# Thirteen blocks of a four-layer kernel turned by block transfers and VectorE instead of TensorE

## The chip, the cores and the metric

The kernel runs on one core of a Trainium2 chip. A core has TensorE (PE: matmuls, with its weight loads shown as PEld), VectorE (DVE), ScalarE (ACT), GpSimd (POOL) and SyncE (SP), whose queue issues most DMAs. The metric is the device time of one execution in microseconds. The kernel before took 1141.09 us, the median of three runs (1140.71 to 1141.46).

## The reference, cut to what matters

The input is 2 sequences of 1024 tokens with 512 channels, all f32. Four layers follow one another, each with a residual sum and a layer normalisation over the channels:

```python
x = layernorm(x + mamba(x, W_in, conv, A_log, D, dt_bias, norm_w, W_out))   # 16 heads of 64, state 16
x = layernorm(x + linear(x, weight, scale))          # product, then a bound on each row's norm
x = layernorm(x + recurrent(x, w_y, w_x, conv, w_ig, w_ag, w_out, ...))     # gated linear recurrence
x = layernorm(x + swiglu(x, gate_w, up_w, down_w, scales))   # integer weights minus 128, 2048 hidden
```

Every layer multiplies x from the right by a weight. TensorE contracts over the partition axis, so each layer needs its input with channels on the partitions ("turned"). The residual sum and the normalisation need tokens on the partitions. So x is turned once per layer.

## The kernel before, in words

The 2048 tokens are four blocks of 512 (`NBLK` = 4, two per sequence). A block of x is kept as a tile of 128 partitions x 4 token groups x 512 channels, 1 MB. Turned, it is 128 partitions x 4 channel groups x 512 tokens.

**Turning.** `transposed` (L232) makes 16 TensorE transposes of 128x128 for a block, four into each of four PSUM banks. ScalarE (L241) or VectorE (L243) copies each bank out. With `split` it writes two pieces instead: ScalarE a rounded fp32r copy (L236) and VectorE the remainder (L237), because the linear layer and SwiGLU run their products as two fast fp32r matmuls in place of one f32 matmul. `by_channel` (L890, L893, L895) does the same for SwiGLU.

**Mamba.** `head(b)` turns block b, makes the small B, C and dt products, starts their convolution (`mix`) and for b > 0 works out the decays by rows (`by_rows`), which go through HBM (`decays`, `since`) and come back broadcast into L. `project(b)` makes the inner products, convolutions and scans (L535); `recur(b)` runs the four chunks (L663, L673, L694); `gates(b)` makes the gate products (L705); `conclude(b)` is the out-projection (L728) with residual and normalisation, and stores the block to `x_mid` in HBM. `weave` mixes one of these as the main line with steps of others: while block b recurs, block b - 1 concludes and head b + 1 runs. Block 0's start, `opening`, is written out by hand and keeps its order on TensorE, VectorE and ScalarE; in it two steps of head 1 are taken.

**Linear.** `linear(b)` loads x from `x_mid` in HBM, turns and splits it into two single-buffered pieces (named wu and wd in the trace, since they share those tags), multiplies (L909), evicts (L913), works out the norm's factor and adds it to x (L933). Blocks 0 and 1 are woven into the last `conclude`, blocks 2 and 3 into the first block of the recurrent layer.

**Recurrent.** `branches(b)` turns x and makes two products (L960) with a convolution and a GELU. `recurrence(b)` makes the two gates (L960, from cv), then a chain of ScalarE, VectorE and GpSimd work that ends in the scan hs (L1025) and y (L1031). `project_back(b)` is its out-projection (L1037) with residual and normalisation. The order is recurrence(b), project_back(b - 1), and the rest of branches(b + 1).

**SwiGLU.** `hidden(m)` makes gate and up products of hidden tile m (L1111, 16 matmuls: 4 channel groups x 2 pieces x 2 weights), then sg (ScalarE, L1118), h (VectorE, L1120), hh (ScalarE, L1126) and hl (VectorE, L1128). `down(m)` adds tile m's 8 down-products (L1134). down(m) is issued after hidden(m + 1). Between blocks, `by_channel(b + 1)` stands between down(14) and down(15). Weights of groups 1 to 3 are loaded and converted by GpSimd (L864) during block 0.

**Order.** Outside the sections ordered by hand the framework's planner orders each engine's instructions: it plays the program through with its own estimates of durations and takes, of what it thinks ready, what comes first in the program. `keep_in_program_order` pins an instruction behind all earlier ones of its engine. Each engine's queue then runs in that fixed order and waits at the first instruction that isn't ready. `reuse_waits="tile"` lets a tile that takes over memory wait for the old tile in that place alone.

Of the kernel before, what the change touches and what calls it, by code (L numbers as in the profile page):

```python
# [37 lines left out]
def model_kernel(ctx: ExitStack, tc: tile.TileContext, t: dict, out: bass.AP):  # L38
# [7 lines left out]
    x_mid = tc.dram_tile([NBLK, P, NJ, D], F32, name="x_mid")  # L46
# [174 lines left out]
    def transposed(pool, b, X, tags=("xT",), split=False, bufs=1, by_act=False):  # L221


        pieces = [
            pool.tile([P, NK, TB], F32R if split else F32, tag=tag, name=f"{tag}{b}", bufs=bufs)
            for tag in tags
        ]
        xT = pieces[0]
        for k in range(NK):
# [5 lines left out]
            if split:  # L235
                nc.scalar.copy(xT[:, k, :], pt)  # L236
                nc.vector.tensor_tensor(  # L237
                    pieces[1][:, k, :], pt, xT[:, k, :].bitcast(F32), ALU.subtract
                )
            elif k % 2 or by_act:  # L240
                nc.scalar.copy(xT[:, k, :], pt)  # L241
            else:
                nc.vector.tensor_copy(xT[:, k, :], pt)  # L243
        return pieces
# [16 lines left out]
    def causal_conv(acc, xpad, w):  # L261

        for k in range(3):
            nc.vector.scalar_tensor_tensor(  # L264
                acc, xpad[:, k : k + TB], w[:, k : k + 1], acc, ALU.mult, ALU.add
            )

# [31 lines left out]
    def started(pm, n, b, row, w, bias, dst, xpad):  # L299
# [10 lines left out]
        def rest():  # L310
            causal_conv(acc[:n, :], xpad[:n, :], w)
            nc.scalar.activation(dst, acc[:n, :], AF.Silu)
# [29 lines left out]
    def head(b, st):  # L342
# [4 lines left out]
        xT = st["xT"] = transposed(mp, b, X, bufs=2, by_act=b > 0)[0]  # L347
# [27 lines left out]
        if b:  # L375
            mix()
# [53 lines left out]
    def by_rows(b, turn, tk):  # L430
# [5 lines left out]
        )  # L436
        if b == 1:
            exponents(*(by_hj[:, i : i + 1] for i in range(1, 5)), pinned=True)
        bias, _, end, rA, rN = (by_hj[:, i : i + 1] for i in range(5))
        nc.vector.tensor_scalar(z, z, bias, None, ALU.add)  # L440
# [140 lines left out]
    def opening(st, own, g, coming):  # L581
# [35 lines left out]
        next(coming)  # L617
# [102 lines left out]
    def conclude(b, st):  # L720
# [27 lines left out]
        nc.sync.dma_start(x_mid[b], X[b])  # L748
# [12 lines left out]
    for b in range(NBLK):  # L761
        if b:
            g, coming = gates(b, st), {}
            fill, plan = conclude(b - 1, before), (0, 0, 2, 0, 2, 0, 2, 2)
            ahead = head(b + 1, coming) if b + 1 < NBLK else iter(())
# [3 lines left out]
        else:  # L769
            turns = (ahead, g, g, ahead, g, g)  # L770
            weave(recur(b, H, st), (next(steps, None) for steps in turns), (2, 2, 1, 1))
# [50 lines left out]
    def later_layers(exact, last=None):  # L822
# [10 lines left out]

        w_f0 = ep.tile([P, NK, D], F32, tag="wF", name="w_f0" + suffix)
        nc.sync.dma_start(w_f0, w_f0_source)
        for b in range(2):
            nc.sync.dma_start(X[b], x_mid[b])
        w1 = wp.tile([P, 5, NK, D], F32, tag="wA", name="w1" + suffix)  # L840
        f0s = par["f0s"] = row("L0_ffn_scale", D, c1, nc.sync, "scale")
        for i, name in enumerate(("w_x", "w_y")):
            nc.sync.dma_start(w1[:, i], w_sources[name])
        nc.sync.dma_start(X[2], x_mid[2])
# [40 lines left out]
        def by_channel(b, X, pieces):  # L885

            for k in range(NK):
                pt = bank("pt")
                for j in range(NJ):
                    nc.tensor.transpose(  # L890
                        pt[:, j * P : (j + 1) * P], X[b][:, j, k * P : (k + 1) * P], ident
                    )
                nc.scalar.copy(pieces[0][:, k, :], pt)  # L893
                if exact:
                    nc.vector.tensor_tensor(  # L895
                        pieces[1][:, k, :], pt, pieces[0][:, k, :].bitcast(F32), ALU.subtract
                    )

        def linear(b):

            xT = transposed(ep, b, X, tags=("wu0", "wd0") if exact else ("wu0",), split=exact)
# [35 lines left out]
            layernorm(X[b], engine=nc.gpsimd)  # L937
            yield

        if last:  # L940
            steps, free = last

            weave(steps, itertools.chain(linear(0), linear(1)), (0, 1, 0, 2, 0, 1, 0, 2, 1))
            free()
        else:
            for _ in itertools.chain(linear(0), linear(1)):
                pass
        nc.sync.dma_start(X[3], x_mid[3])
        for i, name in ((2, "w_ig"), (3, "w_ag"), (4, "w_out")):
# [350 lines left out]
```

## Time and profile before

| what | value |
|---|---|
| median of three runs | 1141.09 us |
| the profiled execution | 1140.83 us |
| its span | 1139.0 us |
| TensorE busy | 1116.2 us, 98% of the span |
| VectorE, ScalarE, GpSimd busy | 677.6, 466.1, 357.8 us |
| granted TensorE clock, mean | 0.998 |
| all transposes of x on TensorE | 256, in 16 groups of 16 |
| HBM read, written | 49.47 MB, 8.68 MB |

A row of the profile names line, engine, operation, output and inputs, shapes and count, then busy time and mean duration. A row of the timeline gives start, duration, engine, line, operation and count; in square brackets stands the idle time before it and what ended it. Matmuls overlap, so a single duration is longer than the step from one to the next.

### The profile page before, as it was taken

The page shows a single profiled execution, that of the slowest core. Times are in us where ns is not written, and L with a number is a line of the kernel's source. Part 1 is how long each engine was busy: PE and PEld are TensorE (multiplying, and loading weights), DVE is VectorE, ACT ScalarE, POOL GpSimd, SP SyncE. Part 2 cuts the span into 40 slices and gives each one's busy share as a digit, 9 for nine tenths or more (in the row PEclk, how much of TensorE's full clock was granted, in tenths as well). Part 3 has the DMA queues.
Part 4 walks back from the last instruction along what each step waited for, and adds up shares of the span by engine and source line. Part 5 has one row for each costly group of instructions (what it writes and reads, how often), then busy time and mean ns, then how long its engine had stood idle before and what let it go on. Part 6 is the DMA issues. An engine that isn't in the chain of part 4 may idle for free.

```text
span 1139.0 us, 12263 instructions
## 1 busy us (share of the span) xinstructions
PE 1116.2 (98%) x4610; PEld 681.3 (60%) x4610; DVE 677.6 (59%) x1226; ACT 466.1 (41%) x714; POOL 357.8 (31%) x347
## 2 busy tenths in 40 slices
PE   8999999999999999999999999999999999999996
PEld 5455445545544655654444444448888888888885
DVE  5997895696769676862707237083328765225224
ACT  3352634453453233566654372543223223223224
POOL 1547461573348240556123212237501001001000
PEclk9999999999999999999999999999999999999999
DMA  9004002401210047112000000003601001000001
GB/s 325 13 16 167 1 1 90 167 0 39 111 71 0 38 173 207 75 47 74 1 1 0 1 0 1 0 1 121 184 1 38 1 1 37 1 1 10 28 1 40
DMA packets 32732, 59.22 MB, mean 52 GB/s; under 512 B 11841, under 2 KB 12641, under 8 KB 30105
## 3 DMA queue, kind: packets, MB, share of 16 engines
q1 hardware_dynamic: 31464, 57.94, 14.6%
q8 instruction: 38, 0.62, 0.2%
q10 hardware_dynamic: 976, 0.39, 0.1%
q14 instruction: 30, 0.24, 0.1%
q0 software_dynamic: 224, 0.02, 0.0%
HBM read 49.47 MB, written 8.68 MB: 51 GB/s over the span
## 4 chain that ended last, share of the span: by engine, by line
PE 84%; DVE 10%; ACT 4%; issue 1%; DMA 1%; SPq 0%; DVEq 0%; ACTq 0%
PE pgu L1111 21%; PE p L960 17%; PE po L1134 10%; PE pg L336 9%; PE px L336 7%; PE po L728 6%; PE po L1037 4%; PE py L663 3%; DVE acc L264 2%; PE po L909 2%; DVE L L535 2%; PE pxt L632 1%; PE pt L232 1%; DVE xc L713 1%; PE py L655 1%
## 5 line engine op out<-in xcount | busy, mean ns | idle before, releaser
L1120 DVE SCALAR_TENSOR_TENSOR h<-pgu,L_ffn_up_scale,sg 128x512 f32<-128x512 f32 x64 | 47.9, 749 | 147.7 <-PE pgu L1111 143.5
L336 PE MATMUL px<-xT,w_in 128*128 128x512 f32 x256 | 114.6, 597 | 0.0
L550 POOL TENSOR_TENSOR L<-L,gm 128x512 f32<-128x512 f32 x64 | 93.5, 1490 | 66.9 <-DVE bdec L545 29.3
L728 PE MATMUL po<-w_out,xc 128*128 128x512 f32 x256 | 112.5, 593 | 2.1 <-DVE L L535 2.1
L336 PE MATMUL pg<-xT,w_in 128*128 128x512 f32 x256 | 113.5, 594 | 0.0
L960 PE MATMUL p<-xT,w 128*128 128x512 f32 x256 | 112.1, 592 | 1.4 <-ACT xT L241 1.4
L960 PE MATMUL p<-cv,w 128*128 128x512 f32 x256 | 111.0, 592 | 0.0
L1134 PE MATMUL po<-wd,hh 128*128 128x512 f32 x256 | 101.3, 396 | 0.0
L1111 PE MATMUL pgu<-wF__4423,wg 128*128 128x512 f32 x256 | 101.2, 396 | 0.0
L1134 PE MATMUL po<-wd,hl 128*128 128x512 f32 x256 | 101.0, 394 | 0.0
L1111 PE MATMUL pgu<-lo__4424,wg 128*128 128x512 f32 x256 | 100.7, 394 | 0.0
L1111 PE MATMUL pgu<-lo__4424,wu 128*128 128x512 f32 x256 | 100.7, 393 | 0.0
L1111 PE MATMUL pgu<-wF__4423,wu 128*128 128x512 f32 x256 | 100.7, 393 | 0.0
L1118 ACT ACTIVATE sg<-pgu,L_ffn_gate_scale 128x512 f32<-128x512 f32 x64 | 44.1, 689 | 132.9 <-PE pgu L1111 132.9
L1126 ACT CAST hh<-h 128x512 fp32r<-128x512 f32 x64 | 39.7, 621 | 117.6 <-DVE h L1120 117.4
L728 PEld LDWEIGHTS po<-w_out,xc 128*128 128x128 f32 x256 | 48.4, 190 | 63.1 <-issue 55.5
L960 PEld LDWEIGHTS p<-cv,w 128*128 128x128 f32 x256 | 48.4, 190 | 59.8 <-issue 58.6
L960 PEld LDWEIGHTS p<-xT,w 128*128 128x128 f32 x256 | 48.4, 190 | 58.8 <-issue 55.3
L336 PEld LDWEIGHTS px<-xT,w_in 128*128 128x128 f32 x256 | 47.6, 190 | 57.6 <-issue 56.7
L1241 POOL TENSOR_TENSOR x<-x,r 128x512 f32<-128x512 f32 x12 | 15.2, 1295 | 206.1 <-DVE r L1240 206.1
L336 PEld LDWEIGHTS pg<-xT,w_in 128*128 128x128 f32 x256 | 47.3, 190 | 54.2 <-issue 53.3
L264 DVE SCALAR_TENSOR_TENSOR acc<-xpad,cols,acc 128x512 f32<-128x512 f32 x72 | 67.5, 941 | 18.5 <-ACT acc L306 14.8
(279 smaller groups left out, 1934.5 us busy)
## 6 DMA issues: line engine op xcount, KB each, us to landing
L<-decays SPq DMA_DIRECT2D x12, 1024.0 KB, 8.3
x_mid<-x SPq DMA_DIRECT2D x4, 1024.0 KB, 3.9
x<-x_mid SPq DMA_DIRECT2D x4, 1024.0 KB, 7.2
st<-in_L_ffn_gate_w_dram SPq DMA_DIRECT2D x8, 512.0 KB, 4.7
st<-in_L_ffn_up_w_dram SPq DMA_DIRECT2D x8, 512.0 KB, 3.9
st<-in_L_ffn_down_w_dram SPq DMA_DIRECT2D x8, 512.0 KB, 3.7
x<-_attn_hidden_states_dram SPq DMA_DIRECT2D x3, 1024.0 KB, 16.6
out_dram<-x SPq DMA_DIRECT2D x3, 1024.0 KB, 4.3
```

The lines of the kernel that those rows point to most:

```text
L264: nc.vector.scalar_tensor_tensor(acc, xpad[:, k : k + TB], w[:, k : k + 1], acc, ALU.mult, ALU.add)
L336: nc.tensor.matmul(pm[:n, :], w_in[:, k, lo : lo + n], xT[:, k, :], start=(k == 0), stop=(k == NK - 1),)
L550: nc.gpsimd.tensor_tensor(L[:, h, :], L[:, h, :], st["gm"], ALU.mult)
L663: nc.tensor.matmul(pys[i][hh * HD : (hh + 1) * HD, q, :], dtx[q][:, 2 * i + hh, :], L[:, h, s], start=(first and q == 0), stop=(q == 1), s ...
L728: nc.tensor.matmul(po, xc[:, m, j * P : (j + 1) * P], w_out[:, m, :], start=(m == 0), stop=(m == NX - 1),)
L960: nc.tensor.matmul(pm, w1[:, i, k, m * P : (m + 1) * P], rhs[:, k, :], start=(k == 0), stop=(k == NK - 1),)
L1037: nc.tensor.matmul(po, y[:, k, j * P : (j + 1) * P], w1[:, 4, k, :], start=(k == 0), stop=(k == NK - 1),)
L1111: nc.tensor.matmul(pm, w[g][:, k, cols], x[:, k, :], start=(k == 0 and x is pieces[0]), stop=(k == NK - 1 and x is pieces[-1]),)
L1118: nc.scalar.activation(sg, pgu[0], AF.Silu, scale=gs[:, m : m + 1])
L1120: nc.vector.scalar_tensor_tensor(h, pgu[1], us[:, m : m + 1], sg, ALU.mult, ALU.mult)
L1126: nc.scalar.copy(hh, h)
L1134: nc.tensor.matmul(po[j], x[:, j * P : (j + 1) * P], wd[m // GK][:, m % GK, :], start=(m == 0 and x is h[0]), stop=(m == NF - 1 and x is h ...
```

## The change

A block that is to be turned is read from HBM by four DMAs (`load_blocks`), one for each 32 partitions, such that every 32x32 square of it already lies in its final place but is not itself turned. Each DMA moves runs of 32 channels, 128 bytes. Then four VectorE instructions (`turn_blocks`), one per channel group of 128 x 512, turn all 32x32 squares. This is done for mamba blocks 2 and 3, all linear blocks, recurrent blocks 1 to 3, and all SwiGLU blocks. Mamba blocks 0 and 1 and recurrent block 0 stay with TensorE. The linear layer and SwiGLU then split from SBUF instead of PSUM. To have the rows in HBM, the outputs of the linear layer (blocks 1 to 3) and of the recurrent layer (all) are stored as well (`x_lin`, `x_rec`).

The recurrent layer's five weights become five tiles, whose places also take the waiting blocks. Gate and up products of SwiGLU's hidden tile 0 are issued before the last `project_back`. In `opening` only one step of head 1 is left; its other steps come at chosen chunks of `recur(0)`, with the first tap of `mix` and the first operation of `by_rows` pinned. The plan that weaves linear 1 is shortened, and its remaining steps go into the first recurrent block.

```diff
-    x_mid = tc.dram_tile([NBLK, P, NJ, D], F32, name="x_mid")
+    x_mid, x_lin, x_rec = (
+        tc.dram_tile([NBLK, TB, D], F32, name=name) for name in ("x_mid", "x_lin", "x_rec")
+    )
...
+    def load_blocks(dst, rows):
+        blocks = rows.rearrange("(n t) (k a c) -> a t k n c", t=32, k=NK, c=32)
+        for a in range(4):
+            nc.sync.dma_start(
+                dst[32 * a : 32 * a + 32].rearrange("t k (n c) -> t k n c", c=32), blocks[a]
+            )
+
+    def turn_blocks(dst, src=None, pinned=False):
+        for k in range(NK):
+            turned = nc.vector.transpose(dst[:, k, :], (src or dst)[:, k, :])
+            if pinned:
+                tc.keep_in_program_order(turned)
...
-        xT = st["xT"] = transposed(mp, b, X, bufs=2, by_act=b > 0)[0]
+        if b > 1:
+            xT = st["xT"]
+            turn_blocks(xT, pinned=True)
+        else:
+            xT = st["xT"] = transposed(mp, b, X, bufs=2, by_act=b > 0)
...
-            mix()
+            mix(b == 1)
...
+        shifted = nc.vector.tensor_scalar(z, z, bias, None, ALU.add)
         if b == 1:
-            exponents(*(by_hj[:, i : i + 1] for i in range(1, 5)), pinned=True)
+            tc.keep_in_program_order(shifted)
+            exponents(*(by_hj[:, i : i + 1] for i in range(1, 5)))
...
         later.pop(0)()
-        next(coming)
         for conv in later:
...
+            if b + 1 < NBLK:
+                by_blocks(b + 1, coming)
+                ahead = head(b + 1, coming)
             weave(project(b, st), fill, plan, rest=False)
...
-            turns = (ahead, g, g, ahead, g, g)
-            weave(recur(b, H, st), (next(steps, None) for steps in turns), (2, 2, 1, 1))
+            turns = (ahead, g, ahead, g, g, g, ahead)
+            weave(recur(b, H, st), (next(steps, None) for steps in turns), (2, 2, 1, 2))
...
+        mid = [staged(ep, "lo", x_mid[0], "mid0")]
         for b in range(2):
-            nc.sync.dma_start(X[b], x_mid[b])
+            nc.sync.dma_start(X[b], rows_mid[b])
+        mid.append(staged(wp, "w3", x_mid[1], "mid1"))
...
-            xT = transposed(ep, b, X, tags=("wu0", "wd0") if exact else ("wu0",), split=exact)
+            x = mid.pop(0)
+            turn_blocks(x)
+            xT = [
+                ep.tile([P, NK, TB], WT, tag=tag, name=f"{tag}{b}")
+                for tag in (("wu0", "wd0") if exact else ("wu0",))
+            ]
+            split(x, xT)
...
-            weave(steps, itertools.chain(linear(0), linear(1)), (0, 1, 0, 2, 0, 1, 0, 2, 1))
+            weave(steps, two, (0, 1, 0, 2, 0, 1, 0, 2), rest=False)
...
-                xT = transposed(rp, b, X, by_act=True)[0]
+                if b:
+                    xT = rp.tile([P, NK, TB], F32, tag="xT", name=f"xT{b}")
+                    turn_blocks(xT, lin.pop(0))
+                    if b + 1 < NBLK:
+                        lin.append(staged(ep, "lo", x_lin[b + 1], f"lin{b + 1}"))
+                else:
+                    xT = transposed(rp, b, X, by_act=True)
...
+            def first_pieces():
+                rec = staged(rp, "xT", x_rec[0], "rec0")
+                yield
+                turn_blocks(rec)
+                ...
+                split(rec, pieces)
+                yield
...
-            weave(branches(0, st), itertools.chain(linear(2), linear(3)), (1,) * 8)
+            weave(
+                branches(0, st), itertools.chain(two, linear(2), linear(3)),
+                (2, 1, 1, 1, 1, 1, 1, 1, 1),
+            )
...
-            by_channel(0, X, pieces)
+            first_hidden = gate_up(0)
             project_back(NBLK - 1, ys[-1])
...
+                    if m == 6 and not final:
+                        load_blocks(following, x_rec[b + 1])
+                    if m == 10 and not final:
+                        turn_blocks(following)
                     down(m, ready.pop(0), po, range(NJ))
...
                     down(NF - 2, ready.pop(0), po, range(NJ))
-                    by_channel(b + 1, X, pieces)
+                    split(following, pieces)
                     down(NF - 1, ready.pop(0), po, range(NJ))
```

`staged` takes a tile from a pool and fills it with `load_blocks`; `split` writes the rounded copy (ScalarE) and the remainder (VectorE) of a turned block; `gate_up(m)` is the product part of `hidden(m)`; `by_blocks` gives a head its tile and its load.

## The prediction

> **What bounds the kernel now.** I read the page first (engine shares, slices, chain), then busy time stage by stage, then the timeline of TensorE around each group of transposes, then VectorE and the transfers.
>
> ```profile
> span 1139.0 us, 12263 instructions
> PE 1116.2 (98%) x4610; PEld 681.3 (60%) x4610; DVE 677.6 (59%) x1226; ACT 466.1 (41%) x714; POOL 357.8 (31%) x347
> ...
> PE   8999999999999999999999999999999999999996
> ...
> PE 84%; DVE 10%; ACT 4%; issue 1%; DMA 1%; SPq 0%; DVEq 0%; ACTq 0%
> ```
>
> TensorE is at work in nearly every slice and holds 84% of the chain that ended last. An instruction taken off TensorE therefore shortens the run, unless it was covering a wait. The busy time by stage shows where that can be (columns: stretch, its length, then busy time and count of PE, weight loads, VectorE, ScalarE, GpSimd):
>
> ```profile
> 100.60:208.60 108.00, 105.28 (x515) 54.31 (x514) 86.61 (x134) 50.02 (x80) 53.64 (x46) 1.00 0.20 78
> 208.60:313.90 105.30, 104.69 (x515) 54.61 (x514) 79.85 (x133) 49.07 (x78) 50.93 (x50) 1.00 0.16 63
> ...
> 414.80:505.60 90.80, 87.99 (x330) 54.60 (x329) 69.95 (x162) 42.98 (x81) 33.80 (x26) 1.00 0.42 131
> 505.60:768.20 262.60, 260.94 (x658) 119.16 (x656) 119.65 (x218) 138.30 (x177) 76.00 (x78) 1.00 0.04 13
> 768.20:1127.00 358.80, 358.80 (x1576) 292.08 (x1575) 159.86 (x302) 102.61 (x154) 50.52 (x55) 1.00 0.10 34
> ```
>
> These are mamba blocks 1 and 2, the linear layer with the end of mamba, the recurrent layer, and SwiGLU. VectorE is 80% and 76% busy in the two mamba stages, 77% in the linear layer, and under half busy in the last two. Work can go to it without a second thought only in those two.
>
> **Part 1, transposes removed.** Thirteen blocks (mamba 2 and 3, linear 0 to 3, recurrent 1 to 3, SwiGLU 0 to 3) lose 16 TensorE transposes each, 208 of 256.
>
> ```profile
> 421.66 0.95 PE L737 MATMUL pss<-ones,sums 128*128 128x1 f32 x8
> 422.47 1.94 PE L232 MATMUL pt<-ident,x 128*128 128x128 f32 x16
> 424.25 7.03 PE L728 MATMUL po<-w_out,xc 128*128 128x512 f32 x16
> ...
> 855.49 0.69 DVE L1128 TENSOR_TENSOR hl<-h,hh 128x512 fp32r<-128x512 f32 x1 [0.69 <-ACT hh L1126]
> 855.64 1.91 PE L890 MATMUL pt<-ident,x 128*128 128x128 f32 x16
> ...
> 857.30 0.47 PE L1134 MATMUL po<-wd,hh 128*128 128x512 f32 x1
> ```
>
> One transpose lasts 273 ns, but they overlap: 16 take 1.91 us, so the step is (1.91 - 0.27) / 15 = 109 ns and a block's group holds TensorE for 16 x 0.109 = 1.75 us. The Trainium skill (VectorE: DVE Perf Modes, The three transpose paths) lists 390 ns for a 128x128 transpose on TensorE and 311 ns on VectorE. By 390 ns the 208 would be worth 81 us; by the step of this trace they are worth 208 x 0.109 = **22.7 us**. I take the trace, since what counts is when the next matmul starts.
>
> **Part 2, what the groups were covering.** In SwiGLU the second fence shows a group that stands between two rounds of down-products. hl of the last hidden tile ends at 855.49 + 0.69 = 856.18; the following down-product needs it and begins at 857.30. Without the group it begins at about 856.2, not at 855.64, so each of the three changes of block gains 1.1 us of the 1.66: **0.55 x 3 = 1.7 us given back**. The new pieces (4 casts, 2.05 us, and 4 subtractions, 2.48 us, as in the trace) still fit behind the 1.86 us of that down-product plus the first products, which need a fourth piece only 1.6 us later.
>
> **Part 3, VectorE turns.** 13 x 4 in-place or copying 32x32 transposes of 128x512. The trace has none. Nearest row: a SBUF to SBUF pass over 128x512 f32, 0.68 to 0.69 us (hl above); at half that rate 1.4 us. I take 0.69 us, 2.8 us a block. Recurrent and SwiGLU: hidden, VectorE idles there 143 and 199 us. Mamba heads 2 and 3: pinned behind the preceding VectorE work, which ends at 170.3 (a normalisation), after which VectorE idles 8.4 us waiting for the head itself; turned by 173.1, and the head's products started at 175.04 anyway. Cost 0 (at 1.4 us: about 1 us a block); the two heads also lose 8 ScalarE copies. Linear: 16 turns add 11.0 us to 69.95, 81 us in a stage that would shrink to some 84 us, so VectorE becomes as tight as TensorE there. Old waits in that stage were 3.4 us (0.3 + 0.6 + 1.6 + 1.0, between 454 and 496). New ones: after linear 1 ends (457.7 with the groups gone) the single-buffered pieces can be rewritten, 0.6 + 0.68 us before the first product, then 0.2 us a piece because VectorE makes them slower than TensorE takes them; about 2 us for that block, about 4 us for VectorE's order. Net **2.5 us given back** (bounds: 3 gained, 7 lost, the stage's whole saving).
>
> **Part 4, transfers.** Each block is read as 4 DMAs of 2048 runs of 128 bytes: 52 more DMAs; 7 more 1 MB stores (x_lin, x_rec); all on SP's queue, where an issue takes 0.3 to 1.2 us, so about 35 us of a queue with over 900 us free.
>
> ```profile
> x<-x_mid SPq DMA_DIRECT2D x4, 1024.0 KB, 7.2
> ...
> L_ffn_up_scale<-in_L_ffn_up_scale_dram SPq DMA_DIRECT2D x1, 8.0 KB, 4.0
> ```
>
> The first line is the same megabyte in long runs; the second is 2048 runs of 4 bytes. Four such in a row, with about 2 us of each fixed (a 32 KB transfer lands in 1.8 to 2.1 us): 4 x 2 + 2 = 10 us. The Trainium skill (DMA: Bandwidth & Descriptors, Why small descriptors are slow, and the 512 B minimum among its specifications) speaks against runs this short; the page on VectorE warns of 19 times for a transpose by strides. Twice the plain 7.2 us would be 14 us; 19 times would be 137 us, and no cover below would hold. I take 10 us, range 7 to 20, because the 4-byte row is the harsher form of the same thing.
>
> Cover: SwiGLU issues at m = 6 and turns at m = 10, 4 x 5.57 = 22 us. Recurrent: a whole block, over 60 us. First SwiGLU block: issued when branch 3 ends (710), needed at 751. Mamba: issued when the old xT is free (100.6, 208.6), used at 170 and 275. If they stand before the loads of L on SP, those (issued 95.6 and 200.7) slip about 15 us against scans that start at 123 and 227; L landed at 109 and 214, so the first group just holds. Mid 0: free to go after the linear weight, 408.5, so landed 419, turned and split behind VectorE's casts by about 429, and needed at 429.3. **Cost 0**; the tightest is mid 0.
>
> **Part 5, waits removed.**
>
> ```profile
> 71.19 0.33 PE L632 MATMUL pxt<-ident,xc 128*128 128x128 f32 x1 [2.44 <-ACT xc L329]
> ...
> 754.73 14.00 PE L1037 MATMUL po<-w,y 128*128 128x512 f32 x32 [1.66 <-DVE r L1042]
> ```
>
> In the opening VectorE ran the second head's taps and softplus (5.5 us from 61.4 to 69.7) between the first block's last taps; the pins put them behind, and the 2.44 us go. What is late next is the second head's decays: two turns later, about 92 instead of 82.3; but the loads of L waited for L itself until 95.6, so that costs nothing. Before the last out-projection, 7.3 us of gate and up products now fill the 1.66 us wait; they add one more change from f32 to f32r, 0.40 us (0.63 instead of 0.23 us at 430.72). **2.4 + 1.7 - 0.4 = 3.7 us.**
>
> **Sum.** 22.7 - 1.7 - 2.5 + 3.7 = 22.2 us. The profiled execution took 1140.83 us (span 1139.0 and 1.8 around it), so 1118.6; the median of the three runs is 0.26 us above it: **1119 us**. Own range 1113 to 1125.
>
> **Rivals.**
> Cover stays: TensorE waits wherever a group went away beside a dependent chain, and VectorE holds up the linear stage. Gains then only where matmuls stood back to back: recurrent 3 x 1.75, mamba 2 x 1.75, 1.7 at SwiGLU's start: 10.5 us, 1130. For it: VectorE's 77% in the linear stage. Against: no wait in TensorE's timeline from 506 to 751.
> Floating turns: only the heads' turns are pinned. The planner lets unpinned work float (the normalisation of X3, written at m = 4, ran at 779.7, m = 1), so VectorE may stand on a load that lands later than planned. A hidden tile has 3.2 us to spare (hl ready 2.4 us after its products, used 5.6 us after), so only the excess counts: some 3 us at each of 3 SwiGLU and 2 linear blocks, 15 us, 1134.
> Slow transfers, ending slower: if a block takes T, mid 0 costs T - 15 and each of the three SwiGLU loads T - 22 (with the turn inside it, a little earlier). At 30 us: 15 + 3 x 8 = 39, 1158. It outweighs the gain from about T = 26, over twice my estimate.
>
> **Chances.** A change of under 0.2% (2.3 us) can't be told from none in this kernel. My forecast 0.62 (and 0.03 for better than 1113), the first two rivals together 0.20 (1125 to 1136), slow transfers 0.12, no difference 0.03 (between the two). Faster 0.85, same 0.03, slower 0.12. The range 1112 to 1136 leaves out the slow case, no difference and the ends.
>
> **What would show it.** 48 TensorE transposes on the line of the tokens' transposes, none in SwiGLU; 52 VectorE transposes near 0.69 us; block loads landing within 14 us; the stretch from 506 to the last out-projection 5 us shorter; SwiGLU's changes of block 1.1 us shorter each; no 2.4 us wait before the first state. Wrong if VectorE or TensorE waits on a block load, or if a turn takes over 1 us in the linear stage.

## The result, and the profile after

The changed kernel takes **1185.14 us** (median of 6 runs, 1181.97 to 1186.03) against 1141.28 us for the kernel before on the same chip: a ratio of 1.0378, with a 95% interval of 1.0362 to 1.0394. It is 44 us slower where 22 us faster was forecast. The profiled execution took 1185.13 us, its span is 1183.1.

The head of the page after, with the busy shares, the slices of TensorE and of its clock, the packets and the chain:

```profile
span 1183.1 us, 12001 instructions
PE 1113.6 (94%) x4402; PEld 667.4 (56%) x4402; DVE 710.5 (60%) x1278; ACT 454.3 (38%) x692; POOL 361.8 (31%) x347
...
PE   8999999999999996388999999998999999999997
...
PEclk9999999999999998689999999998999999999999
...
DMA packets 146827, 80.17 MB, mean 68 GB/s; under 512 B 119280, under 2 KB 120080, under 8 KB 145224
...
PE 72%; DVE 13%; ACT 6%; POOL 3%; SPq 3%; issue 2%; DMA 1%; DVEq 0%; ACTq 0%; POOLq 0%
```

TensorE's work fell as planned (4402 matmuls instead of 4610), but it now stands still in one place, slices 16 to 19 (about 444 to 562 us), and the clock falls there too. The same start and end points in both traces show what each stretch gained or lost:

| point | before | after | lag |
|---|---|---|---|
| first block stored to x_mid | 170.4 | 175.7 | +5.3 |
| third block stored to x_mid | 380.3 | 382.1 | +1.8 |
| first recurrent gate product (L1026, from cv) | 512.5 | 560.0 | +47.5 |
| last recurrent gate product | 737.0 | 781.1 | +44.1 |
| first down-product | 775.9 | 822.4 | +46.5 |
| last down-product | 1129.7 | 1173.9 | +44.2 |

So the opening lost 5.3 us, the two mamba heads gained 3.5, **the linear layer lost 45.7**, the recurrent layer gained 3.4, SwiGLU's start lost 2.4 and its three changes of block gained 2.3.

The busy time by stage (stretch, length, then PE, weight loads, VectorE, ScalarE, GpSimd, the clock, DMA share, GB/s):

```profile
175.70:278.10 102.40, 101.98 (x481) 52.11 (x480) 83.10 (x133) 46.15 (x73) 50.93 (x51) 1.00 0.32 82
...
409.80:456.00 46.20, 43.58 (x118) 22.56 (x119) 22.39 (x34) 9.90 (x16) 10.85 (x7) 0.96 1.17 211
456.00:520.00 64.00, 29.20 (x78) 17.89 (x77) 42.98 (x106) 21.35 (x43) 18.31 (x13) 0.68 0.52 111
520.00:560.00 40.00, 34.85 (x104) 20.06 (x103) 23.80 (x49) 20.19 (x35) 10.23 (x9) 0.96 0.18 44
```

From 456 to 520 TensorE works 29 of 64 us, at a clock of 0.68. VectorE works 43 of 64: it is not full either. Both wait.

TensorE's waits there (start, duration, then in brackets the idle time before and what ended it):

```profile
433.52 1.19 PE L955 MATMUL po<-wfr,wu 128*128 128x512 f32 x4 [2.11 <-ACT wu L932]
...
459.30 0.73 PE L955 MATMUL po<-wfr,wu 128*128 128x512 f32 x2 [2.23 <-ACT wu L932]
463.27 0.80 PE L955 MATMUL po<-wfr,wd 128*128 128x512 f32 x1 [3.24 <-DVE wd L934]
...
478.04 0.69 PE L231 MATMUL pt<-ident,x 128*128 128x128 f32 x2 [8.64 <-POOL x L269]
...
508.07 4.63 PE L1026 MATMUL p<-xT,w 128*128 128x512 f32 x5 [16.21 <-ACT xT L235]
```

SP's queue over the same time (an issue's start and how long SP was held by it), with the scale row's issue before the change in the first line:

```profile
415.83 0.42 SPq L94 DMA_DIRECT2D L_ffn_scale<-in_L_ffn_scale_dram  x1
...
410.24 8.38 SPq L247 DMA_DIRECT2D mid<-x_mid  x4
...
423.26 9.13 SPq L247 DMA_DIRECT2D mid<-x_mid  x4
432.44 1.88 SPq L98 DMA_DIRECT2D L_ffn_scale<-in_L_ffn_scale_dram  x1
...
435.94 14.50 SPq L247 DMA_DIRECT2D mid<-x_mid  x4
```

And VectorE's timeline; the first line is linear 0's first eviction before the change:

```profile
433.17 0.69 DVE L913 TENSOR_TENSOR o<-po,L_ffn_scale 128x512 f32<-128x512 f32 x1 [1.10 <-PE po L909]
...
432.12 2.48 DVE L254 STREAM_TRANSPOSE mid<-mid 128x512 f32<-128x512 f32 x4
...
450.24 0.75 DVE L763 SCALAR_TENSOR_TENSOR x<-po,rms,x 128x512 f32<-128x512 f32 x1 [13.26 <-PE po L748]
457.10 0.75 DVE L763 SCALAR_TENSOR_TENSOR x<-po,rms,x 128x512 f32<-128x512 f32 x1 [6.12 <-PE po L748]
457.77 1.29 DVE L254 STREAM_TRANSPOSE mid<-mid 128x512 f32<-128x512 f32 x2
458.99 2.45 DVE L959 TENSOR_TENSOR o<-po,L_ffn_scale 128x512 f32<-128x512 f32 x4
...
502.29 1.90 DVE L254 STREAM_TRANSPOSE mid<-mid 128x512 f32<-128x512 f32 x3
```

The products of linear 0 were done at 443.3, but their evictions (L959) stand in VectorE's queue behind two residuals of mamba's out-projection (L763), for which VectorE waits 13.26 and 6.12 us; before the change the evictions ran from 433.2. A block's last DMA landed 6.4 to 6.9 us after its issue: mid 1 was there at 437.2 and its turn began at 457.8; mid 2 was there at 455.1 and was turned at 502.3. In the same way ScalarE's copies of xT, whose transposes were done at 487, stand behind casts of linear 2 that wait for that turn. ScalarE's timeline:

```profile
502.37 1.28 ACT L266 ACT_TABLE_LOAD   x1 [7.21 <-DVE mv L264]
...
503.87 2.16 ACT L932 CAST wu<-mid 128x512 fp32r<-128x512 f32 x4
...
507.45 2.03 ACT L235 COPY xT<-pt 128x512 f32<-128x512 f32 x4
```

Nothing in these timelines of TensorE, VectorE and ScalarE waits for a transfer. But the chain of the page does run through SP's block loads here (423.9 to 432.4 and 437.4 to 447.1). Either the transfers made other things late, or the planner put the queues in this order because it takes such loads for later than they are. The experiments ask which.

### The profile page after: what moved, and what is told of

Same layout as the page of the kernel before. It is cut to its first block, busy times and chain, and to the rows that moved or that the text cites. A ratio compares the mean times of both kernels' runs of the same rounds, so it can differ in the third digit from the quotient of the medians.

```text
span 1183.1 us, 12001 instructions
## 1 busy us (share of the span) xinstructions
PE 1113.6 (94%) x4402; PEld 667.4 (56%) x4402; DVE 710.5 (60%) x1278; ACT 454.3 (38%) x692; POOL 361.8 (31%) x347
## 4 chain that ended last, share of the span: by engine, by line
PE 72%; DVE 13%; ACT 6%; POOL 3%; SPq 3%; issue 2%; DMA 1%; DVEq 0%; ACTq 0%; POOLq 0%
PE pgu L1010 19%; PE p L1026 14%; PE po L1213 10%; PE pg L350 8%; PE px L350 7%; PE po L748 4%; PE po L1109 2%; PE py L683 2%; SPq L247 2%; DVE L L556 2%; DVE acc L276 2%; PE po L955 1%; DVE xc L733 1%; PE pxt L652 1%; DVE st L263 1%
## 5 line engine op out<-in xcount | busy, mean ns | idle before, releaser
L1199 DVE SCALAR_TENSOR_TENSOR h<-pgu,L_ffn_up_scale,sg 128x512 f32<-128x512 f32 x64 | 47.8, 748 | 137.7 <-PE pgu L1010 128.0
L1026 PE MATMUL p<-xT,w 128*128 128x512 f32 x256 | 114.9, 607 | 16.2 <-ACT xT L235 16.2
L1026 PE MATMUL p<-cv,w 128*128 128x512 f32 x256 | 111.1, 593 | 1.3 <-DVE cv L276 1.3
L1010 PE MATMUL pgu<-lo__4207,wg 128*128 128x512 f32 x256 | 101.1, 395 | 0.0
L1197 ACT ACTIVATE sg<-pgu,L_ffn_gate_scale 128x512 f32<-128x512 f32 x64 | 44.1, 689 | 130.4 <-PE pgu L1010 130.3
L1026 PEld LDWEIGHTS p<-xT,w 128*128 128x128 f32 x256 | 49.8, 195 | 77.2 <-issue 57.8
L1026 PEld LDWEIGHTS p<-cv,w 128*128 128x128 f32 x256 | 48.5, 190 | 63.2 <-issue 58.8
L556 DVE TENSOR_TENSOR_SCAN L<-pl,id 128x512 f32<-128x512 f32 x64 | 75.0, 1207 | 4.5 <-ACT pl L550 3.5
```

The costliest lines, as they stand in the source:

```text
L556: nc.vector.tensor_tensor_scan(L[:, h, :], pl, id4.rearrange("p j t -> p (j t)"), 0.0, ALU.mult, ALU.add)
L1010: nc.tensor.matmul(pm, w[g][:, k, cols], x[:, k, :], start=(k == 0 and x is pieces[0]), stop=(k == NK - 1 and x is pieces[-1]),)
L1026: nc.tensor.matmul(pm, w1[i][:, k, m * P : (m + 1) * P], rhs[:, k, :], start=(k == 0), stop=(k == NK - 1),)
L1197: nc.scalar.activation(sg, pgu[0], AF.Silu, scale=gs[:, m : m + 1])
L1199: nc.vector.scalar_tensor_tensor(h, pgu[1], us[:, m : m + 1], sg, ALU.mult, ALU.mult)
```

## The experiments

In the expectations the planner is called the scheduler. All ratios are to the kernel before.

**One load moved.** The scale row is issued ahead of the block loads.

```diff
         nc.sync.dma_start(w_f0, w_f0_source)
+        f0s = par["f0s"] = row("L0_ffn_scale", D, c1, nc.sync, "scale")
...
-        f0s = par["f0s"] = row("L0_ffn_scale", D, c1, nc.sync, "scale")
```

> The changed kernel with one load moved: the broadcast row of the linear layer's scale (L_ffn_scale) is issued right after the linear weight, ahead of the block loads of mid 0 and mid 1, instead of behind them; nothing else is edited. Theory A (the load queue): block loads hold SP's queue for some 22 us, the scale row goes out at 432.44 instead of 415.83, so the scheduler puts the evictions of linear 0 behind residuals that wait for the out-projection, and everything after is late. It expects o<-po of linear 0 back near 437 (from 459), the 8.8 us and 16.4 us waits of TensorE at 469 and 491 mostly gone, and a time 20 to 35 us shorter, 1150 to 1165 us. Theory B (the new weave: linear 1's last step taken out of the out-projection's plan and put behind the recurrent layer's first step) expects the 16.4 us wait to stay: at most 10 us shorter, 1175 or more. Theory C (VectorE itself: 16 turns and single-buffered pieces make it the bound of the stage) expects under 5 us, 1180 or more.

1170.68 us, 1.0255 (1.0236 to 1.0275): 14.5 us back, under the 20 that theory A gave at least. The evictions of linear 0 ran from 438.8, but mid 1, there since 438, was turned only at 462.2, and the wait for xT (18 us) stayed. The late row was a part, not the whole.

**The step plans as before.**

```diff
-            weave(steps, two, (0, 1, 0, 2, 0, 1, 0, 2), rest=False)
+            weave(steps, two, (0, 1, 0, 2, 0, 1, 0, 2, 1))
...
-                branches(0, st), itertools.chain(two, linear(2), linear(3)),
-                (2, 1, 1, 1, 1, 1, 1, 1, 1),
+                branches(0, st), itertools.chain(linear(2), linear(3)),
+                (1,) * 8,
```

> The changed kernel with the two step plans of the linear stage as before the change: both first linear blocks run to their end inside the out-projection's plan (0,1,0,2,0,1,0,2,1), and the recurrent layer's first branches are woven with one step each of linear 2 and 3. Block loads, turns and the late scale row stay. Theory A (the load queue) expects little: under 8 us, 1177 or more, since the scale row is as late. Theory B (the weave) expects the 16.4 us wait for xT at 491 to go and 15 to 30 us back, 1155 to 1170. Theory C (VectorE is the bound) expects under 5 us.

1177.56 us, 1.0313 (1.0296 to 1.0331): 7.6 us back. Theory B's 15 to 30 did not come; the wait for xT shrank from 16 to 10 us.

**The exponents pinned.**

```diff
-            exponents(*(by_hj[:, i : i + 1] for i in range(1, 5)))
+            exponents(*(by_hj[:, i : i + 1] for i in range(1, 5)), pinned=True)
```

> The changed kernel with the exponents of the second head pinned again in VectorE's program order, at their new place behind the shift. Theory: unpinned, five tiny instructions float to the front of VectorE's queue and wait there until 11.44 for by_hj, a load of GpSimd's queue, with two copies of xT behind them; TensorE waits 2.65 us at 9.74 and then goes on at half clock. It expects the copies at 8.6, pa at 19.5 instead of 23.7 and a time 4 us shorter, 1181. Rival: the opening's loss of 5 us by the first stored block is due to the reordered turns of the two heads (the decays at 101 instead of 82); then the start gains 4 us but the first stored block doesn't come earlier, and the time stays within 1 us of 1185.

1180.50 us, 1.0339 (1.0319 to 1.0359): 4.6 us back, as the theory had it. VectorE's start in the changed kernel:

```profile
11.44 0.14 DVE L196 TENSOR_SCALAR by_hj<-by_hj 64x1 f32<-64x1 f32 x1 [2.91 <-DMA by_hj<-in_L_attn_A_log_dram]
...
11.76 0.68 DVE L237 COPY xT<-pt 128x512 f32<-128x512 f32 x1
```

And with the pins:

```profile
8.91 0.69 DVE L237 COPY xT<-pt 128x512 f32<-128x512 f32 x1 [0.18 <-PE pt L231]
```

A 64x1 instruction for the second head, which the planner had put first, waited for its load and held up the first block's own copy.

**SwiGLU's first products put back.**

```diff
-            first_hidden = gate_up(0)
             project_back(NBLK - 1, ys[-1])
...
-            ready, check = [hidden(0, first_hidden)], squares()
+            ready, check = [hidden(0)], squares()
```

> The changed kernel with the first gate and up products of SwiGLU put back behind the last out-projection; the pieces still come by transfers and turns. Theory: with the products ahead of it, only one round of gate and up products (3.6 us) stands between the out-projection's last product and the first down-product, but the room of the SwiGLU tiles comes free only when GpSimd has added the last residual (820.05, 7 us behind TensorE): the 6.0 us wait at 816. Put back, two rounds (7.3 us) cover it: the 6.0 us go, the wait of 1.8 us ahead of the last out-projection comes back: 4 us shorter, 1181. Rival: the 6.0 us are due to the turn of the following block, which now stands among VectorE's last residuals (812 to 818); then some 3 us of wait stay at the first down-product and the time is 1184 to 1186.

1181.37 us, 1.0353 (1.0335 to 1.0371): 3.8 us back. The wait before the first down-product fell from 5.86 to 2.03 us and the one before the out-projection came back with 1.51. So theory and rival each have a part, and the theory's reason was not right. VectorE's timeline in the changed kernel:

```profile
818.06 0.65 DVE L1114 TENSOR_TENSOR r<-po,L_attn_b_out 128x512 f32<-128x512 f32 x1
820.09 0.69 DVE L263 BATCH_NORM_STATS2 st<-x 128x6 f32<-128x512 f32 x1 [1.37 <-POOL x L1115]
...
820.91 1.38 DVE L1199 SCALAR_TENSOR_TENSOR h<-pgu,L_ffn_up_scale,sg 128x512 f32<-128x512 f32 x2
```

ScalarE had made the first sg at 809.3, so room was there. What was late is h (L1199), behind a normalisation that waits for GpSimd's last residual. The 7.3 us of gate and up products used to cover that chain; moved up, half of the cover was gone. The turn of the following block, four times 0.68 us among those residuals (812.1 to 818.1), is the likely reason for the 2 us that stay; no run takes it alone away.

**No turns in the linear layer.** This leaves out `turn_blocks(x)` in `linear`; its output differs.

> The changed kernel without VectorE's turns of the four linear blocks: the split reads each block as it was loaded, so the linear layer works on blocks that are not turned and the output differs; the block loads, their place in SP's queue and all else stay. In the run with the scale row first, mid 1 had landed by 438 and was turned at 462.2, mid 2 by 455 and at 488.0: the turns stood in VectorE's queue behind residuals and normalisations. Theory T (the turn's place on VectorE: before the change ScalarE could take a block from TensorE's transposes at once, now its casts wait for VectorE) expects 15 to 30 us back, 1155 to 1170. Theory A (the load queue) expects under 6 us, as the loads are untouched: 1179 or more.

1181.24 us, 1.0332 (1.0315 to 1.0349): 3.9 us back. Theory T falls: it is not VectorE's work of turning.

**Long runs in the linear layer.** The same four tiles (mid 0 shown), filled in one transfer each with 2 KB runs; the output differs.

```diff
+        def whole(pool, tag, rows, name):
+            x = pool.tile([P, NK, TB], F32, tag=tag, name=name + suffix)
+            nc.sync.dma_start(x, rows.rearrange("(j p) d -> p j d", p=P))
+            return x
...
-        mid = [staged(ep, "lo", x_mid[0], "mid0")]
+        mid = [whole(ep, "lo", x_mid[0], "mid0")]
```

> The changed kernel with the four blocks of the linear layer loaded by one transfer of 2 KB runs each instead of four transfers of 128-byte runs; the turns stay, so what is turned is another arrangement and the output differs. Theory A (the load queue) expects at least the 14.5 us that moving the scale row alone brought, and more if the late landing of mid 1 to 3 or of the parameters counts: 1150 to 1170. Theory T (the turn's place on VectorE) expects the same 14 us or so and no more: 1168 to 1172. If even the 14 us stay away, the queue is not what delayed the scale row.

1146.07 us, 1.0032 (1.0019 to 1.0044): **39 us back**, with all turns in place, more than either theory expected. The form of 16 transfers decides. But the form acts in two ways, on the chip and on the planner's order, and the planner chose another order here.

**The linear layer by TensorE.** Its four blocks are transposed and split from PSUM as before, and not loaded as blocks.

> The changed kernel with only the linear layer as before the change: TensorE transposes its four blocks, ScalarE takes them from PSUM, no block loads there; the shortened step plans stay, as do all other parts of the change. Theory A and theory T both expect nearly the whole loss of the stage back (45.7 us between the last mamba product and the first recurrent gate product, less up to 7.6 that the plans hold): 1139 to 1148. If the shortened plans are the main cause, over 1160.

1149.37 us, 1.0054 (1.0037 to 1.0071): 35.8 us back, 1.4 above the expected band. What stays of the stage is the plans: it takes 91.0 us here (first linear product to first recurrent gate product), 81.8 before the change and again 81.8 in the next run, which has the old plans.

**The parts that pay.** The linear layer and its plans as before, exponents pinned, first products back; nine blocks by transfer and turn.

> The parts that seem to pay, without those that seem to cost: block loads and turns for mamba 2 and 3, recurrent 1 to 3 and SwiGLU 0 to 3 as changed; the linear layer and its step plans as before; the second head's exponents pinned; the first gate and up products behind the last out-projection. From the milestones of the two traces: heads 3.5 us gained, opening 0.7 us lost, recurrent layer 3.4, the four SwiGLU blocks 5.0 gained: 1141.3 - 11.2 = 1130, 1127 to 1134. If block loads and turns cost as much elsewhere as in the linear layer, or the gains were borrowed from waits there, 1138 or more.

**1128.84 us, 0.9884 (0.9867 to 0.9900)**: faster than both kernels, and 1 us from the forecast by milestones. The head of its page:

```profile
span 1126.2 us, 12088 instructions
PE 1102.6 (98%) x4466; PEld 665.1 (59%) x4466; DVE 695.4 (62%) x1262; ACT 453.2 (40%) x692; POOL 356.7 (32%) x347
...
PE   9999999999999999999999999999999999999996
...
PEclk9999999999999999999999999999999999999999
```

No slice but the last is below nine tenths: in the mamba, recurrent and SwiGLU layers block loads and turns cost TensorE nothing that shows at this grain. One wait of 2.07 us stays before the first down-product.

**VectorE and ScalarE in written order** in the linear stage: the two `weave` calls stand inside a section ordered by hand.

> The changed kernel with the instructions of VectorE and ScalarE in the linear stage (from the first fill of the last out-projection to the end of linear 3) issued in the order in which the program writes them, instead of the scheduler's; transfers, turns, plans and the late scale row are those of the change. The trace of the changed kernel shows the blocks landed by 423, 437, 455 and 502, but turned at 432, 458 to 462, 502 and 543; with long runs the scheduler chose another order and 39 us came back, without turns only 4. Theory O (the order): the scheduler takes block loads for much slower than they are, so it queues turns, evictions and casts behind work that waits for something else; it expects 25 to 38 us back with the same loads, 1147 to 1160. Theory Q (the transfers themselves: SP's queue held, late rows and blocks) expects under 12 us, 1173 or more.

1176.45 us, 1.0296 (1.0278 to 1.0313): 8.7 us back. This looked like theory Q, but tells little, because the written order makes waits of its own: mid 1 had landed at 435.2 and was turned at 454.3, mid 2 had landed at 453.6 and was turned at 499.3, behind linear 1's sum and normalisation, and TensorE waits 11.67 us for that piece. The last mamba block's late store (474.1, before the change 462.0), which holds up xT, is not the reason: in the chained run below it comes at 476.2.

**The same order with three repairs** (scale row first, exponents pinned, first products back).

> The whole change kept in purpose, with four repairs: the linear stage in written order as in the run before it, the scale row ahead of the block loads, the second head's exponents pinned, the first gate and up products behind the last out-projection. If theory O holds, the linear stage costs no more than with TensorE's transposes and keeps up to 4 x 1.75 us: 1122 to 1132, beside the 1128.8 of the version with TensorE in the linear stage. If theory Q holds, 1140 or more.

1169.12 us, 1.0230 (1.0213 to 1.0248): the repairs bring 7.3 us, the order's own waits stay.

**The opening as before the change**, on top of the version of 1128.84 us.

> The version that left the linear layer and its plans as before (1128.8 us), with the opening of the change undone as well: the second head's first taps unpinned, its exponents pinned ahead of the shift, its step back inside the first block's last convolutions, turns in the old order. In the run with the exponents pinned, the first stored block comes 0.7 us later than before the change, so the reordering gains nothing by itself. It expects 1128 to 1129, no difference over 1 us. If the removed 2.4 us wait of the prediction is worth its time, 1131.

1131.17 us, 0.9902 (0.9886 to 0.9919): 2.3 us slower, so the expectation was wrong. With the old opening the wait of 2.44 us before the first state's transposes is back, with the new one it is 0.44. In the two traces the first block is stored 1.5 us later with the old opening (171.2 against 169.7). Another 1.4 of the 3.0 us between these two traces arise in SwiGLU, whose code is the same in both: there this one has a stretch of half clock at 769.4 and the other none (last section).

**The order of the long runs, with block loads.** All transfers are those of the change. Within the linear stage TensorE's, VectorE's and ScalarE's instructions are chained, without waits for one another's end, in the order that the planner chose in the long-runs kernel.

```diff
+    def in_given_order(start):
+        traced = nc.cur_bb.bb.instructions[start:]
+        for engine, runs in given.items():
+            mine = [i for i in traced if i.engine == engine]
+            order = [mine[k] for lo, hi in runs for k in range(lo, hi)]
...
+            for a, b in zip(order, order[1:]):
+                tc.add_manual_dep(b, a.name, ...)
```

> The changed kernel, all transfers and all work as in it, but with the instructions of TensorE, VectorE and ScalarE in the linear stage chained in the very order that the scheduler chose when the four blocks were loaded in long runs (the run of 1146.1 us). The order written by hand made waits of its own (the last mamba block was stored at 474, before the change at 462), so it could not tell the two theories apart; this one can, since only the transfers' real speed is left as a difference between the two. Theory O (the order chosen for loads that the scheduler takes for slow): 1145 to 1152, and turns right where the blocks have landed. Theory Q (the real transfers: block loads hold SP's queue, so the scale row, the parameters and mid 1 to 3 are late): 1165 or more, with VectorE waiting on a block load or on the scale row. Between them each has its part: of 39 us, what comes back is the order's, the rest the queue's.

1147.57 us, 1.0048 (1.0032 to 1.0064): **37.6 us back, with the slow loads still in place**, and 1.5 us from the kernel with long runs, where the two intervals overlap. SP's queue runs as in the changed kernel, some 2 us later:

```profile
434.35 1.86 SPq L98 DMA_DIRECT2D L_ffn_scale<-in_L_ffn_scale_dram  x1
...
437.83 14.44 SPq L247 DMA_DIRECT2D mid<-x_mid  x4
```

VectorE now meets transfers, and waits for them:

```profile
439.29 1.30 DVE L254 STREAM_TRANSPOSE mid<-mid 128x512 f32<-128x512 f32 x2 [5.33 <-DMA mid<-x_mid]
440.51 2.45 DVE L978 TENSOR_TENSOR o<-po,L_ffn_scale 128x512 f32<-128x512 f32 x4
...
459.83 0.16 DVE L212 SCALAR_TENSOR_TENSOR sp<-L_attn_a_param 128x4 f32<-128x4 f32 x1 [2.59 <-DMA L_attn_a_param<-in_L_attn_a_param_dram]
...
496.95 1.30 DVE L254 STREAM_TRANSPOSE mid<-mid 128x512 f32<-128x512 f32 x2 [4.12 <-DMA mid<-x_mid]
```

These waits cost little against the order: linear 0's evictions follow at 440.5 instead of 459.0. The whole stage's busy time before the change and in the changed kernel:

```profile
430.70:512.50 81.80, 78.99 (x291) 49.19 (x290) 61.01 (x153) 43.55 (x81) 31.19 (x28) 1.00 0.34 97
433.50:560.00 126.50, 86.02 (x241) 50.73 (x242) 71.00 (x160) 43.29 (x81) 28.54 (x22) 0.81 0.51 108
```

And in this one:

```profile
432.40:524.80 92.40, 78.95 (x243) 47.24 (x242) 65.14 (x157) 37.32 (x72) 21.45 (x23) 0.91 0.78 156
```

Theory O holds as to the order: with the same transfers, another order of three engines is worth some 38 of the 44 us. With the order of the long runs, the loads' own speed is worth 1.5 us, which is not clear of noise. Why the planner chose the other order is not shown. What duration it gives such a load is in no trace; that it is too long is inferred from the order, and whether the short runs or the four issues in place of one decide was not tried apart.

**All thirteen blocks, good order.** Exponents pinned, first products back, scale row first, old plans, and the stage chained in the order that the planner gives the same program with long runs (that twin was not timed).

> All blocks turned as in the change, the linear layer's too, with the repairs found: step plans as before, scale row ahead of the block loads, exponents pinned, first gate and up products behind the last out-projection; and TensorE, VectorE and ScalarE of the linear stage chained in the order that the scheduler chooses for the same program when those four blocks come in long runs. Open is what the turns themselves cost in the linear layer once the order is right: 28.0 us of work taken from TensorE in all, 7.0 of it there. If VectorE has room for them, as the prediction's sum had it (2.5 given back, so 4.5 kept): 1122 to 1126, below the 1128.8 of the version with TensorE in the linear stage. If the turns or the late blocks eat what TensorE saves there (in the two runs with the shortened plans, turned blocks with a good order took 1147.6 and TensorE's 1149.4): 1126 to 1129. If real lateness of blocks shows with the tighter plans: over 1131.

1142.78 us, 1.0006 (0.9999 to 1.0013): 14 us slower than with TensorE in the linear layer, the last of the three cases of the expectation. Here transfers are late in earnest. TensorE's timeline, two of its waits:

```profile
466.62 3.89 PE L1045 MATMUL p<-xT,w 128*128 128x512 f32 x5 [7.34 <-ACT xT L235]
...
497.31 0.79 PE L974 MATMUL po<-wfr,wu 128*128 128x512 f32 x1 [4.47 <-ACT wu L951]
```

The first ends as block 3's store has landed (458.5 and 7.4 us; before the change 3.9). The second is for mid 3, for which VectorE waited 14.60 us, by SP's queue:

```profile
458.49 0.37 SPq L241 DMA_DIRECT2D x_mid<-x  x1
...
466.39 0.57 SPq L247 DMA_DIRECT2D mid<-x_mid  x1
478.55 0.37 SPq L241 DMA_DIRECT2D x_lin<-x  x1
478.97 5.52 SPq L247 DMA_DIRECT2D mid<-x_mid  x3
...
490.30 0.71 DVE L254 STREAM_TRANSPOSE mid<-mid 128x512 f32<-128x512 f32 x1 [14.60 <-DMA mid<-x_mid]
```

Block 3 is stored at 458.5, and three of its four loads stand on SP behind the store of linear 1's result, until 479. That is again an order, SP's; how much a better one would save was not tried.

## Why the prediction was wrong, point by point

**The step that failed** is Part 3's "about 4 us for VectorE's order" in the linear stage, and with it Part 4's "Cost 0; the tightest is mid 0". The cost of the loads was measured against their landing time alone, and the loss was bounded by the stage's own saving, as if the rest of the stage kept its order. It did not: the order of three engines hangs on the form of 16 loads, also where the data is there in time, and that order cost 36.7 us.

For the linear stage a saving of 7.0 us with 2.5 given back (at most 7) was forecast. From the third block's store to the first recurrent gate product it took 177.9 us, 132.2 before the change, so 52.7 were given back. The same stretch in other runs divides them:

| run | stretch, us | difference to the row above |
|---|---|---|
| the changed kernel | 177.9 | |
| the same loads, order of the long runs | 141.2 | 36.7, the order |
| long runs | 140.0 | 1.2, the loads' own speed |
| TensorE's transposes, shortened plans | 141.4 | turning saves 1.4 and not 7.0, so 5.6 are missing |
| TensorE's transposes, old plans | 132.2 | 9.2, the shortened plans, which the prediction did not cost at all |

The four parts add up to the 52.7. Each row is one execution, and executions of one of these kernels lie up to 4 us apart, so only the 36.7 and the 9.2 are clear of that. The 9.2 hold for TensorE's transposes: with turned blocks the old plans did not bring them back, and the run with all thirteen blocks took 143.0, in an order of its own. What the turned stage costs in its best order stays open.

The transfers themselves were sized nearly right: mid 0, 1 and 2 had landed 13, 14 and 19 us after their first issue, where 10 (7 to 20) was taken, and each lay there for over 8 us before it was turned. (That is two to three times the plain 7.2 us. The 19 times that the prediction weighed are, on the page it names, against the DMA crossbar's transpose and not against a plain transfer.) Neither sign of being wrong that the prediction named appeared in the changed kernel: no engine's wait is put down to a block load, and no turn took over 1 us. An engine's wait on other engines while its data lies ready was not among them.

**The rival "floating turns"** named the right agent, the planner, and the wrong direction. It expected VectorE to stand on loads that land later than planned, some 15 us. In the changed kernel VectorE stood on other things while the loads lay there. "Slow transfers" named the sign, but its price came from T of 26 us or more; T was 13 to 19.

**Part 1**: right. In the version of 1128.84 us the recurrent layer's stretch between first and last gate product is 219.3 us against 224.5: 5.2, for 3 x 1.75. The two heads gained 3.5, for 2 x 1.75. The step of 109 ns was the right price, not the 390 ns, which the Trainium skill (VectorE: DVE Perf Modes, The three transpose paths) gives for bf16 data, where the data here is f32.

**Part 2**: right in kind; its size is not settled. From the first to the last down-product it took 353.8 us before, 351.5 in the changed kernel and 349.9 in the version of 1128.84 us: 0.8 and 1.3 for each change of block, where 1.1 was forecast.

**Part 3, the turn's size**: right, with 0.67 us for 0.69 taken, and the bound of 1.4 not needed:

```profile
L254 DVE STREAM_TRANSPOSE mid<-mid x16: 668/671/712, 432.1 to 544.5; 128x512 f32<-128x512 f32 x16
```

**SP's queue**: "0.3 to 1.2 us" an issue was wrong, and the trace before already had longer ones (four loads of cw held SP for 8.8 us from 424.4). One of the linear layer's block DMAs holds SP for 1.7 us in the median and up to 9.7, so 8 to 14.5 us for a block of four. The issues of all 52 add up to 100 us in the trace, where about 35 were forecast, the stores included. It made the scale row 17 us late, and held two of the four loads of L (115.6 and 117.6, before 96.9 and 97.7).

**Part 5, opening**: the 2.44 us wait went (0.44 stays), but most of its worth was lost again. With the exponents pinned, the first block is stored 0.6 us earlier than before the change (169.7 against 170.4, in the version of 1128.84 us), not 2.4. Two things were missed. Unpinning the exponents cost 4.6 us; the prediction read the pins that were added and not the one that was taken away. And "about 92, so that costs nothing" was wrong: the decays were stored at 101.1 (96.7 with the exponents pinned) and held the loads of L. The wait at 145 for its scans is 1.95 us instead of 1.02.

**Part 5, SwiGLU's start**: the 1.7 us wait went, and one of 5.9 us took its place. The prediction asked what the products would fill and not what they had been covering where they stood.

## What to carry to other kernels

Where a planner orders the queues by estimated durations, a change of a transfer's form is a change of every order that depends on it: compare the issue order of all engines before looking at bandwidth. If engines wait for one another while the data lies ready, chain the order of a twin kernel with a plainer transfer; it tells order from speed in one run. For each instruction moved or unpinned, ask what it covered where it stood, and what it can now stand in front of.

## What the runs showed of the hardware that was not expected

- **A wait costs more than itself.** After the 5.86 us wait at 816 the granted clock was 0.50 from 822 to 826 and 0.82 from 826 to 830; from 456 to 520 it was 0.68. In the linear stage TensorE was busy 86.0 us for work that takes about 74 at full clock (79.0 before the change, less 48 transposes of 0.109): by this sum some 12 us of the loss are the clock. The Trainium skill (TensorE: Matmul & The Clock Gate, What's actually happening) has the clock halved after an idle window of about 3.4 us; here the shorter waits of the opening (2.38 and 0.47 us) were followed by 0.69 from 16 to 20 as well, and a single one of 1.95 us that ended at 147.3 by 0.50 from 148.2 to 151.5. Nor is it sure to follow: the same wait of 1.95 us in the version of 1128.84 us was followed by 1.00, and its waits of 2.07 and 0.36 us at the first down-products also by 1.00. Almost the same waits (2.05 and 0.36) in the run with the old opening were followed by 0.50 from 769.4 to 772.7.
- **A DMA of 2048 runs of 128 bytes** (256 KB) in the linear stage of the changed kernel landed 6.9 us after its issue in the median of the five whose landing the trace shows (6.4 to 11.1), and held the issuing queue for 0.6 to 9.7 us, 1.7 in the median; one of 1 MB in 2 KB runs held it for 0.36 to 2.2 in the long-runs kernel.
